# Keys and values of six groups as seven block products over shared input sums, in an attention and FFN layer

## The chip, the cores and the metric

The kernel runs on one core of a Trainium2 chip. The metric is the device time of one execution in microseconds (us), as a median of runs. The core has a matrix engine (TensorE, PE in the profile; PEld are its weight loads), three engines for elementwise work (VectorE, DVE; ScalarE, ACT; GpSimd, POOL) and a queue that only issues transfers (SyncE, SP). Each takes its own instructions in order and waits on semaphores for the others. Matmul results go to PSUM, whose banks hold 128 x 512 fp32 values each; all else lies in SBUF.

## The reference

All in fp32. Sixteen sequences of 128 rows and 1024 columns, x, attend to sixteen contexts of the same shape, and an FFN follows:

```python
x = x + xattn(layernorm(x), ctx, ctx)
x = x + ffn(layernorm(x))

# xattn: 32 query heads of 32 columns, 8 heads of keys and values
Q = query @ Wq + bq          # 1024 x 1024
K = key @ Wk + bk            # 1024 x 256
V = value @ Wv + bv          # 1024 x 256
w = softmax(Q K^T / sqrt(32))
y = (w V) @ Wo + bo          # 1024 x 1024

# ffn: a 0/1 kernel, the last fifth of the input columns times -4
out = scale * (x_ei @ kernel)
```

## The kernel before

The sixteen sequences are worked on as eight groups of two (`GB = 2`, groups 0 to 7, T = 256 rows). For each group there are these stages of PE work: keys and values from the context (`prep_k`, `prep_v`), queries (`prep_q`), attention for two sequences and two halves of the heads (`attend`, four a group), the output projection (`out_proj`) and the FFN (`ffn`).

The order of all instructions is fixed when the kernel is built. A class `Stream` keeps an estimated time `now` and a list of generators, each a stretch of dense PE work that yields the estimated us of what it has just issued; `stream.later(us, fn)` issues `fn` when `now` has advanced by so much. In the main loop (L1114 to L1174) group `grp` is attended while the dense stream holds, in this order, the output projection of group `grp - 1`, keys and values of group `grp + 1` (here `nxt`), its queries, and the FFN of group `grp - 1`. So softmax work on DVE and ACT, and the transposes of the probabilities p on PE (`turn`, tpp, L686), are strewn between the dense matmuls. The last `attend` of a group runs the stream until it is empty.

Queries, output projection and FFN are 2 x 2 block products done with seven products instead of eight (`seven`, L549, with the names in `PRODUCTS`, L228). The left and the right operand are halved twice; s1 to s4 and t1 to t4 are sums of blocks. `seven` goes through the seven products with two accumulators: u takes products 1, 3, 5 and 7, one sum upon the other without being cleared; c takes product 2, and v takes products 4 and 6. After each product `read` adds the accumulator to the result on DVE. `ps_mm` has two buffers, so v lies where c lay: product 4 waits for the read of product 2, and product 3, which goes on into u, for the read of product 1. For the queries one block product is 128 columns by 512 rows by 512: 16 matmuls of 128 columns (L538). The weights of a block, or its sums (made once, by POOL, and stored in DRAM), come as pieces of 512 KB, in the order in which they are used (`want`, `fetch`, L234 to L244): a ring of eight buffers, one `fetch` issued on SP after each piece that was used. The input sums (t for queries, s for the output projection) are made by DVE into tiles tagged "comb" (four buffers).

Keys and values are done plainly. `wk_sb` and `wv_sb` (1024 x 256 each) stay in SBUF. `prep_k` (L480) makes two products of 128 key columns by 256 rows, with the weights as the stationary operand, 8 matmuls each of 256 columns, and ACT adds the bias bkT on the way out (kT). `prep_v` (L491) makes two products of 128 rows by 256 value columns, one for each sequence, with the context as the stationary operand, again 8 matmuls of 256 columns each, and DVE adds the bias bv_b (v, L499). Both use `accumulate` (L400), whose matmuls have the line L403; so have those of the queries of group 0.

The context comes transposed by DVE (`turn_ctx`, L430, cT, two halves of four 128-row chunks). The inputs of the queries and of the FFN take the way through DRAM: DVE normalizes them into xq or x2n (L362), SP stores them (dram_x, dram_f, L394) and loads them again block by block (turn_x, turn_f, L391), and DVE transposes blocks of 32 (L456, L868). `convert_ffn` makes the FFN weights' int8 block sums on DVE (L320, sixteen instructions) while groups 1 and 2 are being prepared.

Of the kernel before, what the change touches and what calls it, by code (L numbers as in the profile page):

```python
# [9 lines left out]
FP = mybir.dt.float32  # L10
# [3 lines left out]
AF = mybir.ActivationFunctionType  # L14
# [4 lines left out]
P = 128  # L19
# [4 lines left out]
class Stream:  # L24
# [28 lines left out]
    def run(self, until, keep=lambda: False):  # L53

        while self.now < until or keep():
            while self.events and min(self.events)[0] <= self.now:
                self.fire()
            if not self.piece():
                if not self.events:
                    return  # L60
                at = min(self.events)[0]
                if at > until and not keep():
                    self.now = max(self.now, until)
                    return
                self.now = max(self.now, at)
                self.fire()
# [23 lines left out]
def once(fn, *args):  # L90
    fn(*args)
    yield 0.0
# [3 lines left out]
def kernel(  # L96
# [16 lines left out]
    nc = tc.nc  # L113
    B, S, D = x.shape
    KV = Wk.shape[1]
    F = ffn_w.shape[1]
    HD = 32
# [6 lines left out]
    GB = 2  # L124
# [20 lines left out]
    wf_sb = const.tile([P, 7, NC // 2, F // 2], I8, name="wf_sb")  # L145
    bqT = const.tile([P, NA, NG], FP, name="bqT")
    bkT = const.tile([P, NA], FP, name="bkT")
    bv_b = const.tile([P, KV], FP, name="bv_b")
    bo_b = const.tile([P, D], FP, name="bo_b")
    fscale = const.tile([P, 1], FP, name="fscale")  # L150

# [59 lines left out]
    nc.gpsimd.memset(minus_half, -0.5)  # L211

    nc.gpsimd.dma_start(out=bkT, in_=bk)
    nc.gpsimd.dma_start(out=bv_b, in_=bv.partition_broadcast(P))
    nc.gpsimd.dma_start(out=bqT, in_=bq.rearrange("p (a g) -> p a g", a=NA))
    nc.gpsimd.dma_start(out=fscale, in_=ffn_scale.partition_broadcast(P))
    nc.sync.dma_start(out=bo_b, in_=bo.partition_broadcast(P))
    bqs = const.tile([P, NA, NG], FP, name="bqs")

# [14 lines left out]
    def want(src):  # L234
        feed.append(src)
        return len(feed) - 1
# [15 lines left out]
    def o_block(r, o, k):  # L252
# [6 lines left out]
        for n in range(1, 5)  # L259
        for k in range(2)  # L260
    }

    def want_sum(w, n, k):
        c = 4 if w == "q" else 2
# [139 lines left out]
            if k % 2 == 1 and k < n - 1:  # L404
                yield 2 * rhs.shape[-1] / 600

    cTs, xTs, kTs, vs, qTs = {}, {}, {}, {}, {}

    def turned(store, srcs, grp, h, name, batches=range(GB)):

# [63 lines left out]
    def norm_x(b, then=None):  # L474
# [2 lines left out]
            half_stats(stats, xns[b], k)  # L477
        normalize(xns[b], xns[b], stats, f"a{b}", then)

    def prep_k(grp):  # L480
        kT = work.tile([P, NA, T], FP, tag="kT", name=f"kT{grp}", bufs=2)
        kTs[grp] = kT
        for a in range(NA):
            mm = ps_mm.tile([P, T], FP, tag="mm", name=f"k_{grp}_{a}")
            yield from accumulate(
                mm, [(wk_sb[:, c, a * P : (a + 1) * P], chunk(cTs, grp, c)) for c in range(NC)]
            )
            nc.scalar.activation(kT[:, a], mm, AF.Identity, bias=bkT[:, a : a + 1])
            yield 0.85

    def prep_v(grp, batches=range(GB)):  # L491
        for j in batches:
            b = grp * GB + j
            v = work.tile([P, KV], FP, tag="v", name=f"v{b}", bufs=4)
# [4 lines left out]
            nc.vector.tensor_add(v, mm, bv_b)  # L499
            vs[b] = v  # L500
            yield 0.85

    S4 = [P, NG, S]
# [30 lines left out]
    def product(mm, pairs, start):  # L534

        for n, (part, some) in enumerate(pairs):
            for k, (lhsT, rhs) in enumerate(some):
                nc.tensor.matmul(  # L538
                    mm if part is None else mm[:, part],
                    lhsT=lhsT,  # L540
                    rhs=rhs,
                    start=start and n == k == 0,
                    stop=k == len(some) - 1,
                    skip_group_check=True,
                )
                if k % 2 == 1:
                    yield 2 * rhs.shape[-1] / 600
# [22 lines left out]
    def prep_q(grp):  # L570
# [70 lines left out]

        return run()

    yTs = {}

    def scores(b, a):
        grp, cols = b // GB, slice(b % GB * S, (b % GB + 1) * S)
        qT, kT = qTs[b, a], kTs[grp]
        tiles = [ps_sc.tile([P, NG, S], FP, tag="sc", name=f"sc_{b}_{a}_{i}") for i in range(NI)]
        for g in range(NG):  # L650
            for i in range(NI):
                rows = slice(i * HD, (i + 1) * HD)
                nc.tensor.matmul(  # L653
                    tiles[i][:, g],
                    lhsT=qT[rows, g],
                    rhs=kT[rows, a, cols],
                    start=True,
                    stop=True,
                )
        return tiles  # L660
# [30 lines left out]
    def weighted(b, a, pts):  # L691

        mm = ps_tp.tile([P, NG, S], FP, tag="tp", name=f"av_{b}_{a}")
        for i in range(NI):
            h = a * NI + i
            nc.tensor.matmul(  # L696
                mm[i * HD : (i + 1) * HD],
                lhsT=vs[b][:, h * HD : (h + 1) * HD],
                rhs=pts[i],
                start=True,  # L700
                stop=True,
            )
        yTs[b, a] = work.tile(S4, FP, tag="yT", name=f"yT{b}_{a}", bufs=4)
        nc.scalar.copy(yTs[b, a], mm)  # L704
# [308 lines left out]
    with tc.manual_schedule():  # L1013
# [7 lines left out]
        qs, os = {1: prep_q(1)}, {}  # L1021
        for grp in range(NGRP):
            os[grp] = out_proj(grp)
            if grp + 2 < NGRP:
                qs[grp + 2] = prep_q(grp + 2)

        for _ in range(RING - 2):
# [79 lines left out]
        def between(gen, n, fn, *args):  # L1107

            for i, us in enumerate(gen):
                yield us  # L1110
                if i + 1 == n:
                    fn(*args)

        for grp in range(NGRP):  # L1114
            b0, b1, nxt = grp * GB, grp * GB + 1, grp + 1
            p0, p1 = b0 - 2, b0 - 1
            first, more = grp == 0, nxt < NGRP
            last = grp == NGRP - 1
            length = 17.4 if first else 23.2 if grp < NGRP - 2 else 19.2
            if first:  # L1120
                stream.add(
                    once(norms, nxt, 5.0, 18.0),
                    between(plain(1), 9, sums_of_wq, 0),
                    once(sums_of_wq, 1),
                    prep_k(nxt),
                    once(get_ctx, nxt + 1),
                    prep_v(nxt),
                    prep_x(nxt, 0),
                    prep_x(nxt, 1),
                    once(convert_ffn),  # L1130
                    between(between(qs[nxt], 16, residuals, grp), 24, prep_ctx, nxt + 1, 0.0, 4.0, 8.0, 12.0),
                )
            elif more:
                stream.add(
                    *([once(get_x, nxt)] if grp == 1 else []),
                    once(turn_rows, nxt),
                    os[grp - 1],
                    once(get_ctx, nxt + 1),
                    prep_k(nxt),
                    once(load_residual, b0, 4.0),  # L1140
                    prep_v(nxt),
                    between(qs[nxt], 20, prep_ctx, nxt + 1, 0.0, 5.0, 10.0, 14.0),
                )

# [86 lines left out]
```

## Time and profile before

The median of three runs is 776.85 us (776.61 to 779.83). The profiled execution took 776.96 us on the clock of the runs; its span in the profile is 775.1 us. The granted clock of TensorE was 1.0 throughout.

| engine | busy us | share | instructions |
|---|---|---|---|
| PE | 753.7 | 97% | 4944 |
| PEld | 557.5 | 72% | 4944 |
| DVE | 536.7 | 69% | 947 |
| ACT | 373.7 | 48% | 1361 |
| POOL | 275.6 | 36% | 332 |

| what | figure |
|---|---|
| DMA, all | 192.43 MB, mean 248 GB/s |
| PE k, L403 | 7% of the chain |
| PE v, L403 | 7% of the chain |
| PE q_u, q_v, q_c, L538 | 13%, 7%, 3% of the chain |
| piece<-q on SP | 56 of 512 KB, 7.8 us to landing |
| piece<-o on SP | 64 of 512 KB, 4.5 us to landing |
| piece<-Wq on SP | 50 of 512 KB, 7.5 us to landing |

Busy time is the time with at least one instruction of that engine under way; the chain is followed back from the last instruction to what released each step. A line of the timeline has the start and the length in us, the engine, the line of the kernel, the operation, out<-in, shapes, how many were merged, and in brackets the idle time of the engine before it with what ended it.

### The profile page before, as it was taken

How to read it: one execution, taken by the hardware profiler on the slowest of the kernel's cores; microseconds unless marked ns; L12 is line 12 of the kernel's file. 1: busy time of each engine (PE TensorE's matmuls, PEld its weight loads, DVE VectorE, ACT ScalarE, POOL GpSimd, SP SyncE). 2: the span in 40 equal slices, each digit the busy share in tenths (PEclk: the TensorE clock that was granted, in tenths of full speed). 3: DMA queues.
4: the chain of work that ended last, by engine and by line, in shares of the span. 5: the costliest groups of instructions: out<-in, count | busy, mean ns of one | idle time of the engine just before them, and what ended most of it. 6: DMA issues, size and time to landing. Idle time of an engine off the chain costs nothing.

```text
span 775.1 us, 14162 instructions
## 1 busy us (share of the span) xinstructions
PE 753.7 (97%) x4944; PEld 557.5 (72%) x4944; DVE 536.7 (69%) x947; ACT 373.7 (48%) x1361; POOL 275.6 (36%) x332
## 2 busy tenths in 40 slices
PE   5999999999999999999999999999999999999997
PEld 4877985689747986479855898468974699455375
DVE  2356758887776777658776677865777666778576
ACT  0245764435634455344634437343463455577352
POOL 4078830043720155102650236201272012217652
PEclk9999999999999999999999999999999999999999
DMA  9989999999499876999479895898749967763702
GB/s 246 314 314 276 374 370 366 275 227 305 136 338 247 275 237 204 283 264 285 163 265 262 246 311 164 280 303 238 262 152 320 265 206 236 251 206 110 244 1 109
DMA packets 100870, 192.43 MB, mean 248 GB/s; under 512 B 8560, under 2 KB 58032, under 8 KB 100800
## 3 DMA queue, kind: packets, MB, share of 16 engines
q1 hardware_dynamic: 99024, 189.30, 78.2%
q10 hardware_dynamic: 1248, 1.11, 0.6%
q0 software_dynamic: 528, 1.12, 0.6%
q8 instruction: 39, 0.64, 0.3%
q14 instruction: 31, 0.25, 0.1%
HBM read 161.09 MB, written 30.41 MB: 247 GB/s over the span
## 4 chain that ended last, share of the span: by engine, by line
PE 91%; DVE 5%; DMA 2%; POOL 1%; ACT 1%; issue 0%; SPq 0%; DVEq 0%; POOLq 0%
PE o_u L747 13%; PE q_u L538 13%; PE k L403 7%; PE f_u L902 7%; PE tpp L686 7%; PE v L403 7%; PE o_v L747 7%; PE q_v L538 7%; PE sc L653 5%; PE av L696 4%; PE f_v L902 3%; PE q_c L538 3%; PE o_c L747 3%; PE q L403 2%; PE f_c L902 2%; DVE p L681 1%
## 5 line engine op out<-in xcount | busy, mean ns | idle before, releaser
L669 ACT ACTIVATE p<-sc,negm 128x128 f32<-128x128 f32 x512 | 182.1, 370 | 151.6 <-DVE negm L665 73.6
L342 POOL CAST wide<-wf_sb 128x512 fp32r<-128x512 int8 x154 | 110.1, 753 | 60.7 <-PE f_u L902 59.7
L665 DVE TENSOR_REDUCE negm<-sc 128x4 f32<-128x512 f32 x128 | 87.1, 681 | 56.4 <-PE sc L653 56.4
L688 ACT COPY pt<-tpp 128x512 f32<-128x512 f32 x128 | 75.2, 595 | 89.3 <-PE tpp L686 89.0
L669 ACT ACTIVATION_READ_ACCUMULATOR p<-sc,negm 128x1 f32 x512 | 106.1, 207 | 0.0
L681 DVE TENSOR_TENSOR p<-p,inv 128x512 f32<-128x512 f32 x128 | 101.7, 795 | 4.4
L196 POOL TENSOR_TENSOR x<-x,bo_b 128x256 f32<-128x256 f32 x64 | 54.1, 866 | 95.0 <-DMA x<-in_x_dram 70.7
L538 PE MATMUL q_u<-t,piece 128*128 128x128 f32 x672 | 81.4, 275 | 0.0
L686 PEld LDWEIGHTS tpp<-ident,p 128*128 128x128 f32 x512 | 61.8, 141 | 24.8 <-issue 16.4
L686 PE MATMUL tpp<-ident,p 128*128 128x128 f32 x512 | 75.9, 273 | 3.4 <-DVE p L681 3.4
L538 PEld LDWEIGHTS q_u<-t,piece 128*128 128x128 f32 x672 | 78.0, 192 | 0.2
L403 PE MATMUL v<-wv_sb,cT 128*128 128x256 f32 x256 | 61.2, 387 | 9.3 <-DMA wv_sb<-in_L_xattn_Wv_dram 7.5
L359 POOL TENSOR_TENSOR rs_f<-ve_f,minus_half 128x1 f32<-128x1 f32 x16 | 10.3, 642 | 164.4 <-DVE ve_f L357 164.4
L747 PE MATMUL o_v<-piece,s 128*128 128x512 f32 x128 | 60.7, 601 | 2.2 <-DVE x L761 2.2
L747 PE MATMUL o_u<-piece,s 128*128 128x512 f32 x128 | 59.7, 597 | 0.4 <-DVE x L761 0.4
L403 PEld LDWEIGHTS v<-wv_sb,cT 128*128 128x128 f32 x256 | 47.8, 194 | 15.9 <-DVE cT L430 9.1
L747 PE MATMUL o_u<-piece,yT 128*128 128x512 f32 x128 | 58.6, 599 | 0.0
L403 PE MATMUL k<-cT,wk_sb 128*128 128x256 f32 x256 | 58.0, 380 | 0.0
L403 PEld LDWEIGHTS k<-cT,wk_sb 128*128 128x128 f32 x256 | 47.9, 190 | 8.8 <-issue 2.4
L704 ACT COPY yT<-av 128x512 f32<-128x512 f32 x32 | 18.8, 588 | 71.4 <-PE av L696 71.4
L653 PEld LDWEIGHTS sc<-kT,qT 32*128 32x128 f32 x1024 | 31.5, 186 | 25.7 <-issue 25.7
L340 ACT CAST wide<-wf_sb 128x512 fp32r<-128x512 int8 x70 | 42.4, 631 | 10.5 <-PE f_u L902 10.2
(112 smaller groups left out, 1290.8 us busy)
## 6 DMA issues: line engine op xcount, KB each, us to landing
piece<-o SPq DMA_DIRECT2D x64, 512.0 KB, 4.5
piece<-q SPq DMA_DIRECT2D x56, 512.0 KB, 7.8
piece<-in_L_xattn_Wq_dram SPq DMA_DIRECT2D x50, 512.0 KB, 7.5
piece<-in_L_xattn_Wo_dram SPq DMA_DIRECT2D x48, 512.0 KB, 4.9
xn<-in_x_dram SPq DMA_DIRECT2D x16, 512.0 KB, 4.6
x<-in_x_dram SPq DMA_DIRECT2D x16, 512.0 KB, 4.6
ctx<-in_ctx_dram SPq DMA_DIRECT2D x60, 128.0 KB, 7.0
dram_f<-x2n SPq DMA_DIRECT2D x14, 512.0 KB, 5.2
```

What stands on the lines that cost most here:

```text
L196: lambda cut=cut: nc.gpsimd.tensor_add(x_t[:, cut], x_t[:, cut], bo_b[:, cut]) and None,
L342: nc.gpsimd.tensor_copy(t, wf_sb[:, FFN[name], c])
L403: nc.tensor.matmul(mm, lhsT=lhsT, rhs=rhs, start=k == 0, stop=k == n - 1)
L538: nc.tensor.matmul(mm if part is None else mm[:, part], lhsT=lhsT, rhs=rhs, start=start and n == k == 0, stop=k == len(some) - 1, skip_gro ...
L653: nc.tensor.matmul(tiles[i][:, g], lhsT=qT[rows, g], rhs=kT[rows, a, cols], start=True, stop=True,)
L665: nc.vector.tensor_reduce(negm, tile_, AX.X, ALU.max, negate=True)
L669: nc.scalar.activation(p[:, g], tile_[:, g], AF.Exp, bias=negm[:, g : g + 1], accum_out=total[:, g : g + 1],)
L681: nc.vector.tensor_mul(p, p, inv.unsqueeze(2).to_broadcast([P, NG, S]))
L686: nc.tensor.transpose(tp[:, g], p[:, g], ident)
L688: nc.scalar.copy(pt, tp)
L747: nc.tensor.matmul(mm, lhsT=lhsT[:, 2 * k + c], rhs=w[:, c], start=start and k == c == 0, stop=k == c == 1, skip_group_check=True,)
L902: nc.tensor.matmul(mm, lhsT=part[:, c], rhs=w, start=start and c == n == 0, stop=c == HC - 1 and n == 1, skip_group_check=True,)
```

## The change

Keys and values of groups 2 to 7 are made together by `seven`. The left blocks are the four blocks of the weights (input half by 128 output columns), for Wk and Wv alike; the right blocks are the context's halves by sequence, so the sums t1 to t4 of the context are made once for both. One block product is 4 matmuls for K (weights stationary, context moving) and 4 for V (context stationary, weights moving), all of 128 columns; K goes into columns 0 to 127 of the accumulator and V into 128 to 255. Groups 0 and 1 keep `prep_k` and `prep_v`.

The tiles kT and v become one tile kv (128 x 2 head halves x 2 sequences x {K, V} x 128), and the biases one constant kvb of the same layout without sequences. Of the block sums of the weights s1, s2 and s4 are stored in DRAM and come as pieces, three more per group; s3 overwrites the block a21 of `wk_sb` and `wv_sb`. They are made once, by eight DVE instructions, while group 0 is attended. u4 overwrites the context block b12.

```diff
-    bv_b = const.tile([P, KV], FP, name="bv_b")
+    kvb = const.tile([P, NA, 2, P], FP, name="kvb")
...
+    nc.gpsimd.tensor_copy(kvb[:, :, 0], bkT.unsqueeze(2).to_broadcast([P, NA, P]))
...
+    kv_sums = {n: dram.tile([P, PIECE], FP, name=f"kv_{n}") for n in (1, 2, 4)}
...
+    def kv_weight_sums():
+        temps = {}
+        def sum_(m, n, left, right, op):
+            w = (wk_sb, wv_sb)[m]
...
+            if n == 3:
+                dst = kv_block(w, 1, 0)
+            else:
+                dst = work.tile([P, HC, P], FP, tag="wide", name=f"kvs{m}_{n}", bufs=WIDE)
+                temps[m, n] = dst
+            nc.vector.tensor_tensor(dst, of(left), of(right), op)
+            if n != 3:
+                there = kv_sums[n][:, m * HALF : (m + 1) * HALF].rearrange("p (c n) -> p c n", c=HC)
+                stream.later(4.0, lambda: nc.sync.dma_start(out=there, in_=dst) and None)
+        us = 14.0
+        for args in (
+            (1, "a21", "a22", ADD),
+            (2, "s1", "a11", SUB),
+            (3, "a11", "a21", SUB),
+            (4, "a12", "s2", SUB),
+        ):
+            for m in range(2):
+                stream.later(us, lambda m=m, args=args: sum_(m, *args))
+                us += 2.0
...
+    def prep_kv(grp):
+        ids = {p: want_kv(int(p[1])) for p in PRODUCTS if p[:2] in ("s1", "s2", "s4")}
...
+            for us, *args in (
+                (0.2, 1, "b12", "b11"),
+                (1.0, 2, "b22", "t1"),
+                (4.0, 3, "b22", "b12"),
+                (6.0, 4, "b21", "t2"),
+            ):
+                stream.later(us, lambda args=args: sum_(*args))
...
+            def product_of(prod, mm, start):
...
+                yield from product(
+                    mm.rearrange("p (g n) -> p g n", g=NG),
+                    [
+                        (0, [(wk[:, c], act[:, c]) for c in range(HC)]),
+                        (1, [(act[:, c], wv[:, c]) for c in range(HC)]),
+                    ],
+                    start,
+                )
+                if prod in ids:
+                    fetch()
+
+            def read(mm, c):
+                o, j = int(c[1]) - 1, int(c[2]) - 1
+                dst = kv[:, o, j]
+                other = dst if c in written else kvb[:, o]
+                written.add(c)
+                nc.vector.tensor_tensor(dst, mm[:, : 2 * P].rearrange("p (m n) -> p m n", m=2), other, ADD)
+
+            yield from seven(f"k{grp}", product_of, read)
...
             os[grp] = out_proj(grp)
             if grp + 2 < NGRP:
+                kvp[grp + 2] = prep_kv(grp + 2)
                 qs[grp + 2] = prep_q(grp + 2)
...
                     once(convert_ffn),
+                    once(kv_weight_sums),
...
                     once(get_ctx, nxt + 1),
-                    prep_k(nxt),
-                    once(load_residual, b0, 4.0),
-                    prep_v(nxt),
+                    between(kvp[nxt], 14, load_residual, b0, 4.0),
```

More of the change, by code (lines that the diff above doesn't have):

```diff
@@ L213 @@
     nc.gpsimd.dma_start(out=bkT, in_=bk)
-    nc.gpsimd.dma_start(out=bv_b, in_=bv.partition_broadcast(P))
+    nc.gpsimd.dma_start(
+        out=kvb[:, :, 1], in_=bv.partition_broadcast(P).rearrange("p (a n) -> p a n", a=NA)
+    )
     nc.gpsimd.dma_start(out=bqT, in_=bq.rearrange("p (a g) -> p a g", a=NA))
@@ L261, with want_kv @@
     }
+    kv_sums = {n: dram.tile([P, PIECE], FP, name=f"kv_{n}") for n in (1, 2, 4)}
+    def want_kv(n):
+        return want(lambda: kv_sums[n].rearrange("p (c n) -> p c n", c=1))
     def want_sum(w, n, k):
@@ L405, in accumulate @@
                 yield 2 * rhs.shape[-1] / 600
-    cTs, xTs, kTs, vs, qTs = {}, {}, {}, {}, {}
+    cTs, xTs, kvs, qTs = {}, {}, {}, {}
     def turned(store, srcs, grp, h, name, batches=range(GB)):
@@ L478, in norm_x, with kv_tile @@
         normalize(xns[b], xns[b], stats, f"a{b}", then)
+    def kv_tile(grp):
+        if grp not in kvs:
+            kvs[grp] = work.tile([P, NA, GB, 2, P], FP, tag="kv", name=f"kv{grp}", bufs=2)
+        return kvs[grp]
     def prep_k(grp):
-        kT = work.tile([P, NA, T], FP, tag="kT", name=f"kT{grp}", bufs=2)
-        kTs[grp] = kT
+        kv = kv_tile(grp)
         for a in range(NA):
@@ L487, in prep_k @@
             )
-            nc.scalar.activation(kT[:, a], mm, AF.Identity, bias=bkT[:, a : a + 1])
+            nc.scalar.activation(
+                kv[:, a, :, 0], mm.rearrange("p (j n) -> p j n", j=GB), AF.Identity, bias=bkT[:, a : a + 1]
+            )
             yield 0.85
@@ L493, in prep_v @@
             b = grp * GB + j
-            v = work.tile([P, KV], FP, tag="v", name=f"v{b}", bufs=4)
+            kv = kv_tile(grp)
             mm = ps_mm.tile([P, KV], FP, tag="mm", name=f"v_{b}")
@@ L498, in prep_v @@
             )
-            nc.vector.tensor_add(v, mm, bv_b)
-            vs[b] = v
+            nc.vector.tensor_add(kv[:, :, j, 1], mm.rearrange("p (a n) -> p a n", a=NA), kvb[:, :, 1])
             yield 0.85
@@ L642, in prep_q, with kv_block, of @@
         return run()
+    def kv_block(w, o, r):
+        return w[:, r * HC : (r + 1) * HC, o * P : (o + 1) * P]
+    def kv_weight_sums():
+        temps = {}
+        def sum_(m, n, left, right, op):
+            w = (wk_sb, wv_sb)[m]
+            def of(name):
+                if name[0] == "s":
+                    return temps[m, int(name[1])]
+                return kv_block(w, int(name[1]) - 1, int(name[2]) - 1)
+            if n == 3:
[17 more added lines that the diff above has]
+                us += 2.0
@@ new lines, in prep_kv, with run, sum_ @@
+    def prep_kv(grp):
+        ids = {p: want_kv(int(p[1])) for p in PRODUCTS if p[:2] in ("s1", "s2", "s4")}
+        def run():
+            half = {
+                f"b{h + 1}{j + 1}": cTs[grp, h][:, :, j * S : (j + 1) * S]
+                for h in range(2)
+                for j in range(GB)
+            }
+            kv = kv_tile(grp)
+            def sum_(n, left, right):
+                if n == 4:
+                    t = half["b12"]
+                else:
+                    t = work.tile(S4, FP, tag="comb", name=f"u{n}_{grp}", bufs=4)
+                nc.vector.tensor_tensor(t, half[left], half[right], SUB)
+                half[f"t{n}"] = t
+            for us, *args in (
[5 more added lines that the diff above has]
+                stream.later(us, lambda args=args: sum_(*args))
+            written = set()
+            blocks = {"a11": (0, 0), "a12": (0, 1), "a22": (1, 1), "s3": (1, 0)}
+            def product_of(prod, mm, start):
+                left, right = prod.split()
+                act = half[right]
+                if prod in ids:
+                    piece = pieces[ids[prod]].rearrange("p (m c n) -> p m c n", m=2, c=HC)
+                    wk, wv = piece[:, 0], piece[:, 1]
+                else:
+                    wk, wv = [kv_block(w, *blocks[left]) for w in (wk_sb, wv_sb)]
+                yield from product(
[5 more added lines that the diff above has]
+                    start,
+                )
+                if prod in ids:
+                    fetch()
[6 more added lines that the diff above has]
+            yield from seven(f"k{grp}", product_of, read)
+        return run()
@@ L644 @@
     yTs = {}
     def scores(b, a):
-        grp, cols = b // GB, slice(b % GB * S, (b % GB + 1) * S)
-        qT, kT = qTs[b, a], kTs[grp]
+        qT, kT = qTs[b, a], kvs[b // GB][:, a, b % GB, 0]
         tiles = [ps_sc.tile([P, NG, S], FP, tag="sc", name=f"sc_{b}_{a}_{i}") for i in range(NI)]
@@ L655, in scores @@
                     lhsT=qT[rows, g],
-                    rhs=kT[rows, a, cols],
+                    rhs=kT[rows],
                     start=True,
@@ L694, in weighted @@
         for i in range(NI):
-            h = a * NI + i
             nc.tensor.matmul(
                 mm[i * HD : (i + 1) * HD],
-                lhsT=vs[b][:, h * HD : (h + 1) * HD],
+                lhsT=kvs[b // GB][:, a, b % GB, 1, i * HD : (i + 1) * HD],
                 rhs=pts[i],
@@ L1021 @@
         qs, os = {1: prep_q(1)}, {}
+        kvp = {}
         for grp in range(NGRP):
```

## The prediction

> **What bounds the kernel now.** I read the page first: its busy shares and the chain of waits.
>
> ```profile
> span 775.1 us, 14162 instructions
> PE 753.7 (97%) x4944; PEld 557.5 (72%) x4944; DVE 536.7 (69%) x947; ACT 373.7 (48%) x1361; POOL 275.6 (36%) x332
> ...
> PE 91%; DVE 5%; DMA 2%; POOL 1%; ACT 1%; issue 0%; SPq 0%; DVEq 0%; POOLq 0%
> ```
>
> TensorE (PE) is busy 97% of the span and carries 91% of the chain. So the end moves by the PE time that an edit removes and by the PE idle time that it adds. Other engines count where PE waits for them, which it hardly does: PE's own waits after the first 20 us sum to 8.3 us. Next the chain in order of time, where one steady group (the keys and values of group 5) goes from k through v to q (start, length, what; an fp32 matmul leaves two records, so x28 is 14 matmuls):
>
> ```profile
> 423.43 6.04 PE k L403 x28
> ...
> 436.41 2.59 PE v L403 x12
> 441.10 3.77 PE q_u L538 x32
> 444.87 3.57 PE q_c L538 x32
> ```
>
> A k or v matmul of 256 columns costs 6.04/14 = 0.431 us, a q matmul of 128 columns 3.57/16 = 0.223 us. Last, that stage by engine and VectorE's (DVE's) instructions in it:
>
> ```profile
> 423.30:438.95 15.65, 15.65 (x84) 13.52 (x82) 9.62 (x21) 6.67 (x25) 1.09 (x2) 1.00 0.91 222
> ```
>
> ```profile
> 423.47 0.69 DVE L761 TENSOR_TENSOR x<-o_u,x 128x512 f32<-128x512 f32 x1 [0.61 <-PE o_u L747]
> 424.08 0.68 DVE L665 TENSOR_REDUCE negm<-sc 128x4 f32<-128x512 f32 x1
> 424.68 0.17 DVE L680 RECIPROCAL inv<-total 128x4 f32<-128x4 f32 x1
> 424.88 0.69 DVE L681 TENSOR_TENSOR p<-p,inv 128x512 f32<-128x512 f32 x1
> 425.49 0.69 DVE L351 BATCH_NORM_STATS2 st_f<-x 128x6 f32<-128x512 f32 x1
> 426.09 0.69 DVE L456 STREAM_TRANSPOSE xT<-turn_x 128x512 f32<-128x512 f32 x1
> ...
> 435.15 0.42 DVE L499 TENSOR_TENSOR v<-v,bv_b 128x256 f32<-128x256 f32 x1 [3.03 <-PE v L403]
> ...
> 441.73 0.68 DVE L592 TENSOR_TENSOR t<-xT 128x512 f32<-128x512 f32 x1
> ```
>
> DVE is busy 9.62 of 15.65 us, but unevenly: packed from 420 to 432 us, almost idle after. Within the packed part a 128x512 instruction starts 0.60 us after the one before it, and nothing on PE waits for that, because PE needs DVE only for two v reads.
>
> **The change, part by part.** The saving: per group 32 matmuls of 0.431 (13.81 us) become 56 of 0.223 (12.50 us), 1.31 us less, in six groups 7.9 us. A 128-column matmul has to hide a whole 128x128 weight load as before: the q rows do hide it, for they run at 0.223 us with the same shapes and one load each. The Trainium skill speaks against that ("TensorE: Matmul & The Clock Gate", Part 3, The mechanism): a weight load overlaps running matmuls only where the row group differs, which it never does here, so 24 more matmuls of two loads at its 107 ns would cost an estimated 5.1 us more per group. The q rows decide, and the sum takes their 0.223.
>
> What it adds on DVE per group: four sums u1 to u4 of 128x512 (row 441.73: 0.68 us long, 0.60 to the next), and seven reads of 128x256 from PSUM in place of two (row 435.15: 0.42 long, 0.34 to the next), so 4 x 0.60 + 5 x 0.34 = 4.1 us. ScalarE loses two k reads; it is not on the path, so I count nothing.
>
> What that does to PE. `seven` holds two accumulators (ps_mm has two buffers). Product 3 goes on into u, so it needs the read of product 1; product 4 needs the buffer of product 2, so it needs that read; and so on. In q each read has a product of 3.57 us as cover, here 8 x 0.223 = 1.79 us. DVE takes its queue in order, so I walk it, in the changed program's instruction order, with the steps above. It starts where the page's row starts, at the last read of o_u (423.47): that read 0.61, u1 0.61, negm 0.60, reciprocal 0.20, division 0.61, statistics 0.61, u2 0.61, and only then the read of product 1, from 427.3 to 427.7. PE begins product 1 at 423.4 and has finished product 2 at 427.0. What it costs to start again shows where PE waited for DVE once before (the read it waited for ended at 312.73):
>
> ```profile
> 312.78 1.98 PE L747 MATMUL o_v<-piece,s 128*128 128x512 f32 x4 [0.34 <-DVE x L761]
> ```
>
> Four records take 1.98 us there and 1.72 us without a wait, so a restart costs 0.26. Product 3 therefore begins at 427.7 + 0.3 = 428.0, 1.0 us late. Queued behind the read of product 1 stand a transpose (0.62), a reciprocal and a division (0.81) and a negm (0.60); the read of product 2 ends at 430.1, product 3 at 429.8, so product 4 is 0.6 us late. The two or three transposes of p between products 4, 5 and 6 (0.44 us each) then give DVE room, and I find no third wait: the read of product 3 ends at 432.1 and PE wants it at 433.1. Sum per steady group: 1.6 us of waits against 1.31 saved, +0.3. Both ends: no waits at all, if DVE ran 1 us ahead, -1.3; and 0.5 us more at each of products 3, 4 and 6, if sums beside GpSimd (POOL) work take 1.1 us like the row of 442.44 (1.10) does, +1.8. I take +0.3, for POOL is idle there (1.09 us in the window). Four groups (3 to 6) are alike: +1.1 in all, from -5.2 to +7.
>
> Group 2 (its k stage begins at 145.6) has also the FFN weights' int8 sums in DVE's queue:
>
> ```profile
> 146.40 0.68 DVE L320 TENSOR_TENSOR wf_sb<-wf_sb 128x512 int8<-128x512 int8 x1
> 149.31 0.71 DVE L456 STREAM_TRANSPOSE xT<-turn_x 128x512 f32<-128x512 f32 x1 [0.20 <-DMA turn_x<-dram_x]
> ```
>
> Four of them stand between the last read of o_u and the reads that PE waits for. The same walk gives waits of 1.5, 1.1 and 1.3 us ahead of products 3, 4 and 6: 3.9 - 1.3 = +2.6 (from 0 to +5; the second row shows the transpose of turn_x waiting 0.20 for its DMA, and here every later read stands behind that transpose). Group 7 (608.5) has other work between its products: one wait of 1.2 us ahead of product 4, so -0.1 (from -1.3 to +1.5).
>
> The sums of the weights: eight DVE instructions of 128x512, 0.6 to 1.75 us each (1.75 is the t row at 85.93, while POOL works on the weight sums), spread over q of group 1, where DVE idles 1.9 us before 99.72, 1.8 before 102.17 and 2.9 before 114.20. Three fall into those gaps; the others push the last division of that attention step from 110.6 to about 113.5, and its transpose on PE is due at 114.0. I take +0.5, from 0 to +3. Six stores of 256 KB go into SP's queue between the fetches of wo; the eight like them beside (o<-wo) took 7.5 us there, and the first `out_proj` uses its pieces from 117.5 on, so this is in the same +3.
>
> DMA per group: three pieces of 512 KB more on top of about 23 MB (192 MB over eight groups). The ring keeps eight pieces ahead as before and the turn_x loads keep their place in SP's queue. But the first x2n (L362) comes 4 us later, behind the new DVE work, and the second store to dram_f is now queued behind the first's reload, with q's last pieces behind both:
>
> ```profile
> 438.36 1.58 SPq L394 DMA_DIRECT2D dram_f<-x2n  x2
> 443.31 1.74 SPq L391 DMA_DIRECT2D turn_f<-dram_f  x4
> 445.15 0.38 SPq L243 DMA_DIRECT2D piece<-q  x1
> 445.62 1.80 SPq L391 DMA_DIRECT2D turn_f<-dram_f  x4
> 447.52 1.48 SPq L243 DMA_DIRECT2D piece<-q  x3
> ```
>
> Before, the two stores went together at 438.4 and the pieces at 447.5. Now the second store goes at about 446, its reload waits 5 us for it, and q's 11th piece goes at 454, is wanted at 461, and takes 4.5 to 7.8 us. That is just in time; the cover of some 10 us has gone. I take 0.2 us for each of five groups, +1.0, from 0 to +8. The FFN's own blocks are safe: their DVE transposes stand behind a read of q_v in either order. The constants (kvb in place of bv_b) land before 15.6 us, and PE needs the first v read at 18.2: nothing.
>
> **Sum.** 2.6 + 1.1 - 0.1 + 0.5 + 1.0 = +5.1 us. The profiled execution took 776.96 us (span 775.1 and 1.9 around it), 0.1 above the median of 776.85. So 782.
>
> **The rivals.**
> 1. DVE keeps up. If the read of product 1 ends before product 2 does (427.0, 0.7 us earlier than in my walk), most waits vanish and the saving stands: about 0.4 us of waits a group, 5 x 0.9 saved in groups 3 to 7, nothing in group 2: 772.5, and 769 with no wait at all. For it: DVE is 40% idle in the stage. Against it: the idle time lies after 432 us, and the order of the queue is fixed.
> 2. Late pieces. If q's 11th to 14th pieces come 1.5 us late in five groups, 7.5 us replace my 1.0, and with the upper half of the waits (+2) it is 790. For it: DMA is at 0.91 to 1.07 of its engines' time in this stage. Against it: nothing waits for a piece in the trace of before.
> 3. A draw. Waits of 1.3 us in every group, group 2 included, cancel the saving: 777.
> 4. It does not do what it says: loads that do not hide behind 128 columns. The q rows speak against it, but there the weights and the moving operand do not change roles every four matmuls as here. If 24 more loads of 0.192 us (the mean of PEld in L538) lay open, that would be 4.6 us more a group, 28 in all: 805, far outside. I give it 0.02 of rival 2's 0.14.
>
> **How the numbers follow.** The forecast (small loss, 778 to 786) has 0.46, of which 0.10 below +0.5%; rival 1 has 0.23, rival 2 with 4 has 0.14, rival 3 has 0.17. A measurement tells 0.5% (3.9 us) from no change. So faster 0.23, same 0.27, slower 0.50. The likeliest case's own range is 778 to 786. The range for 8 in 10 reaches down to 770.5, into most of rival 1, and up to 791, into half of rival 2.
>
> **What would show it.** In the changed profile: the kv matmuls at 0.223 us each (4 records in 0.45); PE waits in the kv stage put down to the read from k_u and k_c at the start of products 3 and 4, about 1.0 and 0.6 us, longest in group 2; a kv stage of some 15.9 us against 15.6; q's last pieces landing near their use. It is wrong if PE shows no waits there (then rival 1), if idle PE time is put down to a piece (rival 2), or if single matmuls are slower (rival 4).

## The result and the profile after

The changed kernel takes 782.82 us (median of five runs, 782.14 to 784.87) against 776.85 (775.97 to 779.83) for the kernel before on the same chip: ratio 1.0077, 95% interval 1.0052 to 1.0101, some 6 us slower. The profiled execution took 784.87 us, with a span of 782.9; it is the slowest of its five, so its difference to the profile of before (7.8 us of span) is larger than that of the medians.

The page of the changed kernel, parts 1 and 4 (busy time, share and instructions of each engine; the chain of waits):

```profile
span 782.9 us, 14836 instructions
PE 751.9 (96%) x5232; PEld 563.8 (72%) x5232; DVE 563.4 (72%) x1009; ACT 366.2 (47%) x1349; POOL 273.3 (35%) x333
...
PE 76%; DVE 12%; DMA 8%; POOL 1%; issue 1%; ACT 1%; SPq 0%; DVEq 0%; POOLq 0%
```

PE has less to do than before (751.9 us instead of 753.7), and the span is longer: PE now waits. Its share of the chain fell from 91% to 76%; DVE (5 to 12%) and DMA (2 to 8%) took it over. The k and v stage of group 5 shows the first place. PE's rows in the timeline:

```profile
431.01 1.06 PE L551 MATMUL k_c<-wv_sb,cT 128*128 128x128 f32 x8
432.82 1.16 PE L551 MATMUL k_u<-u,piece 128*128 128x128 f32 x8 [0.75 <-DVE kv L747]
433.81 1.06 PE L551 MATMUL k_u<-piece,u 128*128 128x128 f32 x8
435.15 0.71 PE L551 MATMUL k_v<-u,piece 128*128 128x128 f32 x4 [0.28 <-DVE kv L747]
```

and DVE's:

```profile
428.54 0.69 DVE L868 TENSOR_TENSOR x<-o_u,x 128x512 f32<-128x512 f32 x1 [0.61 <-PE o_u L854]
429.14 0.68 DVE L710 TENSOR_TENSOR u<-cT 128x512 f32<-128x512 f32 x1
...
431.76 0.67 DVE L710 TENSOR_TENSOR u<-cT,u 128x512 f32<-128x512 f32 x1
432.35 0.42 DVE L747 TENSOR_TENSOR kv<-k_u,kvb 128x256 f32<-128x256 f32 x1
...
434.69 0.41 DVE L747 TENSOR_TENSOR kv<-k_c,kv 128x256 f32<-128x256 f32 x1
```

Four matmuls (x8 records) start 0.89 us apart where nothing stops them. So product 2 was over at 431.01 + 0.89 = 431.90, and product 3 began at 432.82, right behind the end of DVE's read of product 1 (432.35 + 0.42). Its first four matmuls then last 0.99 to the next start instead of 0.89: 1.02 us lost. In the same way product 4 comes 0.55 us late, behind the read of product 2. In group 2 the same rows carry three waits:

```profile
151.66 1.16 PE L551 MATMUL k_u<-u,piece 128*128 128x128 f32 x8 [1.35 <-DVE kv L747]
...
154.60 0.71 PE L551 MATMUL k_v<-u,piece 128*128 128x128 f32 x4 [0.89 <-DVE kv L747]
...
160.69 1.16 PE L551 MATMUL k_v<-cT,piece 128*128 128x128 f32 x8 [0.95 <-DVE kv L747]
```

By starts that is 1.6, 1.2 and 1.2 us. The whole k and v stage of group 5, by engine (length, then busy time and instructions of PE, PEld, DVE, ACT, POOL, clock, DMA share, GB/s):

```profile
428.34:444.16 15.82, 14.79 (x129) 14.41 (x128) 13.66 (x30) 5.70 (x23) 1.10 (x2) 1.00 1.05 270
```

PE is idle 1.03 of 15.82 us; DVE went from 9.62 to 13.66 us. The second place is the output projection, where nothing was changed. In the main loop the output projection of a group runs while the next group is attended, so the five that lose are those of groups 1 to 5; the recorded expectations below number the same stages by the group that is attended ("groups 2 to 6", "group 6"), except that of group 0. The output projection of group 5 lost 1.56 us. In the timeline of the kernel before, POOL adds bo_b to the next x (L196) around its two rs_a (the scale of the normalization), which DVE's xq needs; the first addition and the first rs_a:

```profile
583.74 0.73 POOL L196 TENSOR_TENSOR x<-x,bo_b 128x256 f32<-128x256 f32 x1 [6.28 <-DVE mv_a L355]
584.42 0.55 POOL L359 TENSOR_TENSOR rs_a<-ve_a,minus_half 128x1 f32<-128x1 f32 x1
```

In the changed kernel two additions stand ahead of the first rs_a, and they wait for x's DMA:

```profile
591.75 1.41 POOL L196 TENSOR_TENSOR x<-x,bo_b 128x256 f32<-128x256 f32 x2 [8.56 <-DMA x<-in_x_dram]
593.11 0.55 POOL L367 TENSOR_TENSOR rs_a<-ve_a,minus_half 128x1 f32<-128x1 f32 x1
593.63 0.73 POOL L196 TENSOR_TENSOR x<-x,bo_b 128x256 f32<-128x256 f32 x1
```

```profile
593.70 1.21 DVE L370 TENSOR_SCALAR xq<-xn,mv_a,rs_a 128x1024 f32<-128x1024 f32 x1 [1.06 <-POOL rs_a L367]
```

```profile
596.70 0.63 PE L794 MATMUL tpp<-ident,p 128*128 128x128 f32 x4 [0.44 <-DVE p L789]
...
602.55 1.98 PE L854 MATMUL o_u<-piece,s 128*128 128x512 f32 x4 [0.82 <-DVE x L868]
```

So DMA holds POOL, POOL's rs_a holds DVE's xq for 1.06 us (and xq itself takes 1.21 instead of 0.80), the division and the reads behind it come late, and PE waits twice. The stage lengths of the profiles, group by group, put the difference to the profile of before like this (starts of stages subtracted; "again" is a second profile of the changed kernel, run e12 below; "adds" is e9, the run with the additions moved):

| part | predicted | after | again | adds |
|---|---|---|---|---|
| groups 0 and 1, up to q of group 1 | 0 | 0.6 | 0.3 | 0.6 |
| sums of the weights (q of group 1) | 0.5 | 0.4 | 0.0 | -0.1 |
| k, v, q of group 2 | 2.6 | 2.7 | 2.7 | 2.7 |
| k, v, q of groups 3 to 6 | 1.1 | 1.0 | 1.0 | 1.0 |
| k, v, q of group 7 | -0.1 | 0.8 | 0.8 | 0.8 |
| late pieces of q | 1.0 | 0 | 0 | 0 |
| output projections of groups 1 to 5 | 0 | 3.2 | 1.7 | -0.4 |
| FFN and the end | 0 | -0.9 | -1.0 | -1.0 |
| sum, to the last FFN's start | 5.1 | 7.7 | 5.5 | 3.6 |

No run here explains the first row, nor the gain in "FFN and the end" (five FFNs 0.1 us shorter each, the last output projection 0.4 to 0.5).

### The profile page after: what moved, and what is told of

Read it like the earlier page. It is cut to its first block, busy times and chain, and to the rows that moved or that the text cites. A ratio compares the mean times of both kernels' runs of the same rounds, so it can differ in the third digit from the quotient of the medians.

```text
span 782.9 us, 14836 instructions
## 1 busy us (share of the span) xinstructions
PE 751.9 (96%) x5232; PEld 563.8 (72%) x5232; DVE 563.4 (72%) x1009; ACT 366.2 (47%) x1349; POOL 273.3 (35%) x333
## 4 chain that ended last, share of the span: by engine, by line
PE 76%; DVE 12%; DMA 8%; POOL 1%; issue 1%; ACT 1%; SPq 0%; DVEq 0%; POOLq 0%
PE q_u L551 12%; PE o_u L854 10%; PE f_u L1009 7%; PE q_v L551 7%; PE tpp L794 6%; PE o_v L854 5%; PE sc L761 4%; PE av L803 4%; PE f_v L1009 3%; PE q_c L551 3%; PE k_v L551 3%; PE o_c L854 3%; PE k_u L551 3%; DMA turn_x<-dram_x 2%; PE q L411 2%; DVE p L789 2%
## 5 line engine op out<-in xcount | busy, mean ns | idle before, releaser
L350 POOL CAST wide<-wf_sb 128x512 fp32r<-128x512 int8 x154 | 108.4, 743 | 61.0 <-PE f_u L1009 60.4
L196 POOL TENSOR_TENSOR x<-x,bo_b 128x256 f32<-128x256 f32 x64 | 52.8, 846 | 79.0 <-DMA x<-in_x_dram 71.8
L761 PEld LDWEIGHTS sc<-kv,qT 32*128 32x128 f32 x1024 | 31.4, 186 | 25.7 <-issue 25.7
L953 POOL TENSOR_TENSOR s<-turn_f,turn_f 128x512 f32<-128x512 f32 x7 | 9.3, 1325 | 99.7 <-DVE turn_f L975 69.1
L854 PEld LDWEIGHTS o_u<-piece,yT 128*128 128x128 f32 x128 | 23.5, 190 | 28.4 <-issue 26.7
L854 PEld LDWEIGHTS o_u<-piece,s 128*128 128x128 f32 x128 | 23.0, 190 | 28.0 <-issue 22.0
L854 PEld LDWEIGHTS o_v<-piece,s 128*128 128x128 f32 x128 | 22.3, 190 | 26.6 <-issue 18.2
```

Source lines behind the costliest of these rows:

```text
L196: lambda cut=cut: nc.gpsimd.tensor_add(x_t[:, cut], x_t[:, cut], bo_b[:, cut]) and None,
L350: nc.gpsimd.tensor_copy(t, wf_sb[:, FFN[name], c])
L761: nc.tensor.matmul(tiles[i][:, g], lhsT=qT[rows, g], rhs=kT[rows], start=True, stop=True,)
L854: nc.tensor.matmul(mm, lhsT=lhsT[:, 2 * k + c], rhs=w[:, c], start=start and k == c == 0, stop=k == c == 1, skip_group_check=True,)
```

## The experiments

Runs with the same figure under "before" shared a chip and its runs of the kernel before.

| run | median us | before | ratio, 95% interval |
|---|---|---|---|
| e1_early_sums | 775.93 | 777.53 | 0.9980, 0.9967 to 0.9993 |
| e2_u2_twice | 786.03 | 777.53 | 1.0108, 1.0090 to 1.0126 |
| e3_group2_plain | 781.21 | 777.53 | 1.0042, 1.0027 to 1.0058 |
| e4_before_and_dma | 778.60 | 777.53 | 1.0015, 1.0003 to 1.0026 |
| e5_early_and_ffn | 777.27 | 777.44 | 1.0001, 0.9986 to 1.0016 |
| e6_and_turns | 775.59 | 777.44 | 0.9985, 0.9972 to 0.9998 |
| e7_before_tweaked | 778.71 | 777.44 | 1.0019, 1.0011 to 1.0028 |
| e8_pool_sums | 776.49 | 777.44 | 0.9985, 0.9974 to 0.9996 |
| e9_adds_alone | 781.21 | 776.81 | 1.0058, 1.0046 to 1.0069 |
| e10_pool_all | 774.83 | 776.81 | 0.9981, 0.9965 to 0.9997 |
| e11_all | 773.88 | 776.81 | 0.9977, 0.9956 to 0.9998 |
| e12_after_again | 784.48 | 776.81 | 1.0099, 1.0085 to 1.0113 |

**Is it the order of DVE's queue?** Two sums earlier, and one sum more.

```diff
-                (0.2, 1, "b12", "b11"),
-                (1.0, 2, "b22", "t1"),
                 (4.0, 3, "b22", "b12"),
...
+            stream.later(0.2, lambda: sum_(1, "b12", "b11"))
+            stream.later(3.0, lambda: sum_(2, "b22", "t1"))
+        begins[grp] = begin
...
-                    os[grp - 1],
+                    between(os[grp - 1], 9, begins[nxt]),
```

> The changed kernel, with the sums u1 and u2 of groups 2 to 7 issued while the output projection before them still runs, two places and four places earlier in VectorE's queue; nothing else moves. Theory (the order of VectorE's queue sets the waits ahead of products 3 and 4): the read of product 1 ends some 1.2 us earlier, so the wait ahead of product 3 goes to about 0 in groups 3 to 7 and halves in group 2. That is 4 x 1.3 + 1.2 + 1.4 = 7.8 us less than 782.8, so 775 (774 to 777), and in group 5 no wait over 0.3 us on a read from k_u. Rival A (the waits come from a lasting shortage of VectorE time, so an earlier sum only moves the wait into the output projection or to a later product): 781 to 784. Rival B (the loss is DMA, not VectorE): 782 to 784 with the waits gone.

```diff
-                nc.vector.tensor_tensor(t, half[left], half[right], SUB)
+                for _ in range(2 if n == 2 else 1):
+                    nc.vector.tensor_tensor(t, half[left], half[right], SUB)
```

> The changed kernel with the sum u2 written twice, one more 128x512 instruction (0.60 us to the next) ahead of the read of product 1 in VectorE's queue, in six groups. Theory (that read sets when product 3 begins): each group's wait ahead of product 3 grows by 0.6, 6 x 0.6 = 3.6 us, so 786.4 (785.5 to 787.5); in group 5 the wait of 0.75 becomes about 1.35. Rival A (VectorE has slack and the waits have another cause): 782.5 to 783.5, the wait the same.

Both medians lie in the ranges of the first theory: 775.93 us, and 786.03. With the sum written twice PE's row in group 5 is

```profile
434.20 1.16 PE L551 MATMUL k_u<-u,piece 128*128 128x128 f32 x8 [1.48 <-DVE kv L748]
```

so 1.48 instead of 0.75: one more instruction of 0.60 in front of the read costs PE 0.73, and the k and v stages of all six groups are 0.72 to 0.73 us longer than in the changed kernel. There is no slack there. The profiles carry this and not the medians, since the two runs of the changed kernel (ratios 1.0077 and 1.0099) lie further apart than the nearer of them and this one (1.0108). With the two sums early product 3 waits for nothing, and product 4 keeps a remainder:

```profile
427.42 1.06 PE L551 MATMUL k_u<-u,piece 128*128 128x128 f32 x8
428.31 1.06 PE L551 MATMUL k_u<-piece,u 128*128 128x128 f32 x8
429.47 0.71 PE L551 MATMUL k_v<-u,piece 128*128 128x128 f32 x4
```

429.47 is 0.27 us behind 428.31 + 0.89, and 0.10 more goes in the restart. In group 2 the wait only moved: 0.15 in place of 1.35 ahead of product 3, but 1.80 in place of 0.89 ahead of product 4, where the int8 sums still stand. That the median came so near the theory's 775 is partly luck: by the profiles the k and v stages became 6.2 us shorter than in the changed kernel and not 7.8, two q stages lost 0.9 of that again, and the output projections of groups 1 to 5 lost 0.3 us where the two profiles of the changed kernel have 3.2 and 1.7, which this theory doesn't speak of.

**Group 2 alone.** Group 2 takes `prep_k` and `prep_v` again, without its three pieces; the third weight sum is moved.

```diff
-                stream.later(us, lambda m=m, args=args: sum_(m, *args))
+                if args[0] == 3:
+                    late.append(lambda m=m, args=args: sum_(m, *args))
...
-                kvp[grp + 2] = prep_kv(grp + 2)
+                if grp:
+                    kvp[grp + 2] = prep_kv(grp + 2)
...
-                    between(kvp[nxt], 14, load_residual, b0, 4.0),
+                    *(
+                        [
+                            prep_k(nxt),
+                            once(load_residual, b0, 4.0),
+                            prep_v(nxt),
+                            once(lambda: [f() for f in late] and None),
+                        ]
+                        if nxt == 2
+                        else [between(kvp[nxt], 14, load_residual, b0, 4.0)]
+                    ),
```

> The changed kernel with group 2's keys and values computed as before the change, as 32 matmuls of 256 columns; groups 3 to 7 as changed, and the third weight sum moved behind group 2's values, since it overwrites a block that group 2 needs. Theory (group 2 loses 2.7 us because the int8 sums of the FFN's weights stand in VectorE's queue there): 782.8 - 2.7 = 780.1 (779.3 to 781). Rival (group 2's waits only move a delay that comes anyway, and the FFN behind it takes it up): 782.5 to 783.5.

781.21 us is just above the range. In ratios to the kernel before it is 1.0042 against 1.0077 and 1.0099 of the two runs of the changed kernel, 2.7 to 4.4 us less; in its profile k, v and q of group 2 lose 1.2 us instead of 2.7, 0.92 of it a new wait of PE for qT in q. The direction is the theory's; the size isn't fixed by it.

**The added DMA by itself.** In the kernel before, two fetches in `prep_k` and one in `prep_v` of groups 2 to 7 bring three pieces that nobody reads.

```diff
             nc.scalar.activation(kT[:, a], mm, AF.Identity, bias=bkT[:, a : a + 1])
+            if grp > 1:
+                fetch()
...
+                for _ in range(3):
+                    want_sum("q", 1, 0)
```

> The kernel before the change with three pieces of 512 KB more, which nobody reads, fetched in the k and v stage of each of groups 2 to 7: the change's added DMA alone, 9.4 MB. Theory (VectorE's and GpSimd's order makes the whole loss, the DMA nothing): 776.9 to 777.9. Rival (the added DMA makes the losses of some 3 us in the output projections, by later loads of x): 779 to 781, with those losses in the output projections of groups 3 to 6.

778.60 us lies between the two ranges: 1.2 us slower (0.2 to 2.0 by the interval). The largest wait of PE that its profile adds is for a piece:

```profile
183.60 2.05 PE L542 MATMUL q_u<-t,piece 128*128 128x128 f32 x16 [0.93 <-DMA piece<-q]
```

The output projections of groups 1 to 5 show +0.5, -0.5, 0, 0 and +0.5. So the DMA alone costs about a microsecond, and doesn't make the 3.2.

**Taking the rest away.** First the int8 sums, then also the transposes:

```diff
-                4.5 * n + 2.5 * m,
+                33.0 + 1.7 * m,
```

> The kernel of the first run (u1 and u2 early), and the sixteen int8 sums of the FFN's weights finished during the output projection of group 0, so that none stands in VectorE's queue in group 2's k and v stage. In the first run that stage lost 0.3, 2.0 and 1.1 us ahead of products 3, 4 and 6. Theory (the int8 sums ahead of the reads are late, not the pieces): at most 0.4 of the 3.4 stays, 775.9 - 3 = 772.9 (772.3 to 774). Rival (the waits go back to the output projection of group 0, where VectorE then has the sums and its reads together): 775 to 777, with PE waits on reads of o_u, o_c or o_v between 110 and 145 us.

```diff
-            for n, at in enumerate((30.0, 32.0, 34.0, 36.0)):
+            for n, at in enumerate((32.0, 34.0, 36.0, 38.0) if grp > 1 else (30.0, 32.0, 34.0, 36.0)):
```

> The run before, and the four transposes of turn_x issued 2 us later in groups 2 to 7, so that none stands between the reads of products 1 and 2. In the first run 0.37 us remained ahead of product 4 in group 5, with one transpose of 0.63 between those reads. Theory (still the order): those 0.37 go in groups 3 to 6 and 2, 1.5 to 1.9 us less, 771.2 (770.5 to 772). Rival (the transposes are then late for q, whose first products need them): 773 or more, with PE waits on q_u or on the t sums.

The first missed: 777.27, no better than the run with early sums, as its rival has it. The sums now stand ahead of a read in group 0's output projection; the rows of DVE and of PE:

```profile
132.44 1.28 DVE L328 TENSOR_TENSOR wf_sb<-wf_sb 128x512 int8<-128x512 int8 x2
...
135.99 0.68 DVE L873 TENSOR_TENSOR x<-o_v,x 128x512 f32<-128x512 f32 x1
```

```profile
136.73 1.98 PE L859 MATMUL o_v<-piece,s 128*128 128x512 f32 x4 [0.98 <-DVE x L873]
```

That stage lost 1.24 us, and group 2's k and v stage stayed 1.5 us behind those of groups 3 to 6 (a wait of 0.51 ahead of product 2 among it). The second did what it was made for (0.37 us in each k and v stage of groups 3 to 6 are gone, the stage is 3.51 shorter than before where the run before had 3.14), yet 775.59 is far from the 771.2 expected, and not by its rival's late transposes: PE doesn't wait for q's inputs. Its profile has the output projection of group 5 losing 1.46 us again.

> The kernel before the change with the same two moves (int8 sums in group 0's output projection, transposes 2 us later): a control, whether these help without the change. Theory (the kernel before has no waits there, so nothing is to be won): 776 to 778. Rival (the moves are good for either kernel): below 775, and then a gain of the two runs above is not the change's.

The control, with the last two diffs on the kernel before, is 1.5 us slower (0.9 to 2.2) and at 778.71 above the range of its theory too, so these moves bring nothing of themselves; the int8 sums cost the same 1.24 us in group 0's output projection.

```diff
-                nc.vector.tensor_tensor(t, half[left], half[right], SUB)
+                (nc.gpsimd if n < 3 else nc.vector).tensor_tensor(t, half[left], half[right], SUB)
```

> The changed kernel with u1 and u2 of every group made by GpSimd instead of VectorE, at the same places. GpSimd takes 0.73 us for 128x256, so about 1.5 for each sum, and is idle there. Theory (two instructions fewer in VectorE's queue ahead of the read of product 1): like the first run, 776 (775 to 777.5). Rival (GpSimd beside VectorE stretches VectorE's instructions, as the 1.10 us instead of 0.68 beside an addition of x suggest, or the sums are late themselves): 779 to 783, with VectorE's instructions of 128x512 above 0.9 us in the k and v stage, or PE waits on u from GpSimd.

776.49, like the early sums: taking the two sums off DVE's queue does the same as moving them up in it. The k and v stages of groups 3 to 6 are 3.14 us shorter than before here too.

**The output projections.** The four additions are moved behind both rs_a:

```diff
-                6.0 + us * k,
+                first + us * k,
...
-            return lambda j: load_residual(b, us) if j == 0 else None
+            return lambda j: load_residual(b, us, first=12.5 if us == 2.0 else 6.0) if j == 0 else None
```

> The changed kernel with one move: GpSimd's four additions of bo_b to the next x are issued 6.5 us later in the output projections of groups 2 to 6, behind both rs_a instead of two before the first rs_a and one between them. Theory (the additions wait for x's DMA and hold up rs_a, VectorE's xq behind it and the read of the output projection behind that): the output projections of groups 2 to 6, which lost 3.2 us in the profiled execution of the changed kernel and 0.3 to 1.9 in others, lose nothing: about 1.2 less than the unchanged copy in this call, 781.6 (780.5 to 782.3). Rival (those losses are the DMA's own and come in any order): within 0.5 of the copy.

> All moves together with GpSimd making u1 and u2: int8 sums earlier, transposes 2 us later, additions of bo_b behind both rs_a. VectorE then has neither u1 nor u2 in the output projection of group 0, where 1.2 us were lost with u1 and u2 early. Theory (the waits are all of order): the full 7.9 us of the products less 0.8 in group 7, 0.7 that the int8 sums still cost and 1.2 of DMA, 776.9 + 1 - 7.9 + 2.7 = 772.7 (771.5 to 774.5). Rival (from here on late pieces and loads decide): 775 to 777, with PE waits on pieces.

> The same with u1 and u2 on VectorE, early: 774.4 (773 to 775.5), some 1.2 us less than the same without the later additions (775.6); its output projection of group 6 loses at most 0.2 where it lost 1.46. Rival (the additions are not the cause): 775 to 776.5, and group 6 loses over a microsecond again.

> The changed kernel itself, for the same chip as the three runs before: 782 to 784. Theory: the waits in the k and v stages are the same to 0.1 us as in its first profile (order, not chance), while the losses in the output projections differ by a microsecond and more in sum, since they hang on when x's DMA lands.

The second run of the changed kernel (e12, the copy) took 784.48 us, a little over its range; with the additions moved (e9) it is 781.21, 3.3 us less, more than the 1.2 expected, and no execution of the copy is as fast as the slowest of e9. The two profiled executions, the copy's fastest and e9's slowest, differ by 1.9. With the additions moved the output projections of groups 3 to 5 lose 0.04 us each and those of groups 1 and 2 nothing. The move takes two things away at once, the wait of rs_a and the addition that ran beside xq (0.81 us here, 1.21 before the move); what each is worth wasn't told apart. The copy's waits in the k and v stages agree with those of the first profile to 0.01 us in every group, while its output projections lose 1.7 us and not 3.2.

The run with all moves and DVE sums (e11) shows that a late x alone costs nothing: POOL's order is needed as well. Its SP rows and POOL rows in the output projection of group 5:

```profile
572.26 0.34 SPq L1043 DMA_DIRECT2D out_dram<-x  x1
577.56 0.33 SPq L190 DMA_DIRECT2D x<-in_x_dram  x1
```

```profile
580.17 0.55 POOL L367 TENSOR_TENSOR rs_a<-ve_a,minus_half 128x1 f32<-128x1 f32 x1 [6.48 <-DVE ve_a L365]
583.23 1.07 POOL L367 TENSOR_TENSOR rs_a<-ve_a,minus_half 128x1 f32<-128x1 f32 x1 [2.51 <-DVE ve_a L365]
584.27 3.75 POOL L196 TENSOR_TENSOR x<-x,bo_b 128x256 f32<-128x256 f32 x4
```

x's load is issued 5.30 us after the store of the tile that it takes over (5.34 in the changed kernel, 5.38 in the run with early sums and moved transposes, 3.13 in the kernel before), so it is as late as ever; but rs_a waits only for DVE, and the stage loses 0.04 us where the same kernel without this move (e6) lost 1.46. The order alone costs nothing either: the run with early sums (e1) has the two additions ahead of the first rs_a too, its load is issued 3.28 us after the store, and this stage loses 0.04 us. Where the order is that of the change, the loss grows with the lateness: 0.7 to 0.8 us in five of six output projections with 4.0 to 4.6 us between store and load, 1.1 to 1.6 in all four with 5.0 to 5.4. The load goes when the store has landed (3.1 us after its start in the kernel before, 5.3 in the changed one). Why the store takes longer in some places stays open: over 4 us occur in 11 of the 55 output projections of groups 1 to 5 in the profiles with the change, in none of the 15 without it, and with the added DMA alone it is 3.1 at most.

All moves together give 773.88 us with DVE sums, inside the range of its theory and 0.23% under the kernel before (0.02 to 0.44), and 774.83 with POOL sums, between its theory and its rival. With POOL sums the output projection of group 0 loses 1.25 us although neither u1 nor u2 stands in DVE's queue there; so the int8 sums alone make that loss, as in the control, and its theory was wrong there. The groups' products now save what was worked out (in groups 3 to 6 k and v are 3.5 us shorter, of which 2.2 come back in q, where attention work has moved to). What keeps the gain at 2 to 3 us: 1.24 us for the int8 sums in group 0's output projection, 1.3 in group 2's k and v stage (2.2 with POOL sums), the 0.8 of group 7, and late pieces. PE waits 0.34 us for a piece in one group of the profile of the one, 0.56 in the other, and likewise 0.41 and 0.50 with early sums alone and with the int8 sums moved; the profiles of e6 and e8 have no such wait. The runs of these kernels also lie wide apart (772.0 to 779.4 for the DVE version; 780.4 to 781.6 with only the additions moved). Their longer executions weren't profiled, so it stays open whether late pieces make them longer.

## Why the prediction was right, and where it was not

**The saving.** 0.223 us a matmul was right: four matmuls take 0.89 us with every weight new, and the weight loads (mean 0.19 us, two records to a matmul) stay hidden. The Trainium skill's rule ("TensorE: Matmul & The Clock Gate", Part 3, The mechanism), that a load overlaps a running matmul only where the row group differs, would have added an estimated 5.1 us a group; these rows show none of it.

**The walk through DVE's queue.** The main step, and right nearly to the tenth: in steady groups 1.02 and 0.55 us against 1.0 and 0.6, in group 2 1.6, 1.2 and 1.2 against 1.5, 1.1 and 1.3, in group 7 one wait of 1.3 ahead of product 4 against 1.2. The stage of some 15.9 us came out at 15.82. Adding an instruction, moving two, or giving them to POOL changed the waits as the order says (0.73 us for an instruction of 0.60). Rival 1 (DVE keeps up) is what the early sums make of the k and v stages of groups 3 to 7; rival 3 had the waits of group 2 too low.

**The failed term "late q pieces, +1.0".** Nothing of it came: PE waits for no piece in either profile of the changed kernel. The order on SP came as I had walked it. My times were on the clock of the profile before, in which group 5's stage begins 5.07 us earlier (423.27 against 428.34); on that clock the second store went at 446.0, as worked out:

```profile
447.98 2.96 SPq L399 DMA_DIRECT2D turn_f<-dram_f  x4
451.03 0.38 SPq L402 DMA_DIRECT2D dram_f<-x2n  x1
451.51 1.26 SPq L246 DMA_DIRECT2D piece<-q  x2
454.34 1.79 SPq L399 DMA_DIRECT2D turn_f<-dram_f  x4
456.23 1.08 SPq L246 DMA_DIRECT2D piece<-q  x2
```

But its reload went 3.3 us behind it and not 5, so the 11th piece went at 456.23, which is 451.2 where I had 454. It took 8.4 us to land, at 464.6, and PE comes to it at 466.07, without a wait:

```profile
466.07 2.84 PE L551 MATMUL q_v<-xT,piece 128*128 128x128 f32 x24
```

That leaves 1.5 us of the cover: the wait of the reload was the mis-sized step. Of the six kernels with u1 and u2 early or on POOL, four have a wait of 0.3 to 0.6 us for a piece at this product in one group, and the added DMA by itself has one of 0.9 at another. So rival 2 had a mechanism that exists, but not at the size that it needs here.

**The failed term "the sums of the weights, +0.5".** 0.4 in one profile and 0.0 in the second; the kernel before with more DMA and no such sums has 0.5 in the same stretch. Nothing that a profile can tell from no cost.

**The failed step "group 7, -0.1".** The wait was right; the loss is 0.8 all the same. The rows of the end of its q stage, before and after:

```profile
655.67 0.60 PE L686 MATMUL tpp<-ident,p 128*128 128x128 f32 x4
656.11 1.06 PE L538 MATMUL q_u<-t,piece 128*128 128x128 f32 x8
657.10 1.06 PE L696 MATMUL av<-pt,v 128*32 128x512 f32 x8
```

```profile
663.90 0.60 PE L794 MATMUL tpp<-ident,p 128*128 128x128 f32 x4
664.43 1.85 PE L803 MATMUL av<-pt,kv 128*32 128x512 f32 x8
```

Before, four q matmuls lie between the last transpose and `av`, while ACT copies pt (the copy starts 0.69 us behind the transposes in both). Now the dense work has run out one place earlier, `av` follows at once and takes 1.78 us to the next start instead of 0.99. I had counted the products and not what is strewn between them. The q stage is the same 0.8 longer in all eleven profiles with seven products in group 7. The cause is read from these rows alone: no run here tried to mend it.

**The step that was missing: POOL's queue in the output projections.** I had walked DVE, SP and PE past the moved work, and POOL only inside the k and v stage. The change alters the estimated times at which things are issued, so two additions came ahead of the first rs_a instead of one. They wait for x's DMA: 1.7 to 3.2 us by the two profiles, 3.3 by the medians with and without the move. Nothing in the sum of 5.1 us stands for these stages. That the first run came to 782.82, so near 782, is therefore partly luck (the copy lost 7.7 us to the kernel before and not 6.0): terms of 1.5 us didn't come, 0.9 us of group 7 and 2 to 3 us of output projections were not foreseen, and some 1 us was gained in the FFNs and at the end without being foreseen either.

**A small slip.** The DMA of the kernel before is 24 MB a group (192.43 over eight) and not 23; nothing rests on it.

## What to carry to other kernels

When work is put on an engine that "has room", walk its queue in order up to the instruction that the bottleneck waits for: here the busy share (61% of the stage) said nothing, and the walk gave the waits to a tenth of a microsecond. Then walk every queue whose order the edit shifts, in stages that it doesn't touch too, and look for an instruction that waits for a transfer in front of a small one that the critical engine needs. And count what lies between two dependent steps of the bottleneck: work taken out of a stage is also cover taken away.

## What the runs showed of the hardware

In group 5 a restart of PE behind a read on DVE cost more than what the profile names as the wait: four matmuls started 0.89 us apart, product 3 started 0.92 us later than that for a named wait of 0.75, and 0.10 more went in its first four matmuls. Summing the waits that the profile names gives too little here: 1.03 us in that stage, where the starts show 1.57.

The store of an x tile took 2.6 to 3.4 us to land in nine of the fourteen profiles and 4.6 to 5.4 in the five others, at the same place in the queue (the output projection of group 5). The load into the same tile was issued within 0.1 us of that landing each time.
